# Selective scan: the sum over states on TensorE as accumulating transposes, and relu in place in PSUM

## The chip, the core and the metric

The kernel runs on one core of a Trainium2 chip. The metric is the device time of one execution in microseconds (us), as the median of several runs. The core's engines work side by side, each through its own queue of instructions in order: TensorE (PE in the profile, with PEld for its weight loads), VectorE (DVE), ScalarE (ACT), GpSimd (POOL) and SyncE (SP), which issues nearly all DMAs here. SBUF is the on-chip memory of 128 partitions; PSUM is the smaller memory that TensorE writes its results to.

## The reference, cut to what matters

Four layers work on x of 256 x 256 positions and 128 channels. Layer 1 holds the selective scan that the change is about: for each of 4 directions k, 256 inner channels d and 16 states n, a recurrence over all L = 65536 positions.

```python
delta = jax.nn.softplus(dts + dt_bias[None, :, :, None])
def step(h, inp):
    d_t, x_t, B_t, C_t = inp
    dA = jnp.exp(d_t[..., None] * As)
    h = dA * h + (d_t * x_t)[..., None] * B_t[:, :, None, :]
    y = jnp.einsum('bkdn,bkn->bkd', h, C_t)
    return (h, y)
...
return ys + Ds[None, :, :, None] * xs
```

y is thus a sum over the 16 states of h times C, plus a multiple of x. The directions are row by row, column by column, and each of these backwards; their outputs are added later.

## The kernel before, in words

The scans (`scan_stream`, L577) come third in the kernel: layer 0 and a convolution come before them, the layer's end, layer 2 and layer 3 after. The work is cut into N = 512 chunks of CH = 512 positions, 128 for each direction. Channels lie on partitions, in two halves dh = 0 and 1. A chunk has NG = 8 steps s, one group g of scans each: s % 2 is the half dh, and s // 2 picks G = 4 of the 16 states.

What one group needs, and who does it:

- `scans` (L770): twice per group, ACT computes the two exponentials of a pair of states (L786) into one of two PSUM buffers `das`, corrects the column at the seam of the pair with the state kept from the chunk before (L790), and DVE runs one scan over 1024 elements (L801) into the SBUF tile h, of which there are 3. After the first scan of a group ACT keeps the last group's states (`keep_state`, L812).
- `b_product` (L768): delta times x times B, on POOL for j in (2, 4, 6), else on DVE. The table `b_order` says in which step each stands.
- `c_product` (L816): POOL multiplies h by C into hc, of which there are 3.
- `sums` (L829 to 837): TensorE adds up the states. Four matmuls per group with the identity as the stationary operand accumulate hc[:, i] in the PSUM tile ys[dh], 128 x 512. A matmul in fp32 is two PE instructions in the trace. `y_start` (L819) opens the accumulation with the multiple of x (directions 0, 1) or with the output of the opposite direction (2, 3). `sums(g - 2)` stands after the scans of group g.
- `y_out` (L844): ACT copies the finished ys[dh] to the block yo in SBUF, which a DMA stores.

The next chunk's delta is made beside this in one PSUM tile, mm, first for dh = 0 and then for dh = 1: `xproj` (L672) and `dt` (L704) are matmuls; `soft_abs` (L716, L717) takes |v| and relu(v) from mm to SBUF; `soft_exp` (L723, L724) turns |v| into log(1 + exp(-|v|)); `soft_sum` (L730) adds the two parts in mm with two identity matmuls; `delta_copy` (L738) takes the result to SBUF; `delta_x` (L746) multiplies it by x on DVE; `du_copy` (L757) keeps a copy for POOL.

The order is written by hand under `manual_schedule`. Small pieces of ACT work, the "extras", are put behind the first (extras[0]) or the second scan (extras[1]) of a step; ACT's queue is in order, so extras[0] stands ahead of the exponentials of the step's second scan. In step 1 extras[1] is soft_abs and y_out of half 0 of the chunk before; in step 2 extras[0] is soft_exp and extras[1] is y_out of half 1.

The attention of layer 0 uses 128x128 fp32 transposes on TensorE (L341), with the data as the stationary operand and the identity streaming.

Of the kernel before, what the change touches and what calls it, by code (L numbers as in the profile page):

```python
# [10 lines left out]
F32 = mybir.dt.float32  # L11
AF = mybir.ActivationFunctionType
# [5 lines left out]
P = 128  # L18
S = 256
NPOS = S * S  # L20
CH = 512
# [555 lines left out]
def scan_stream(c, xc2, y, w):  # L577
# [7 lines left out]
    tc, nc = c.tc, c.nc  # L585
    G, BL, NG = 4, 1024, 8
# [8 lines left out]
    N = len(chunks)  # L595
    with ExitStack() as a:
# [3 lines left out]
        wk = a.enter_context(tc.tile_pool(name="l1b_wk", bufs=2))  # L600
# [9 lines left out]
        ys = [ps1.tile([P, CH], F32, name=f"l1b_y{dh}") for dh in range(2)]  # L610
# [2 lines left out]

        mm = ps1.tile([P, CH], F32, name="l1b_mm")
        du1 = ps1.tile([P, CH], F32, name="l1b_du")
        blocks, bcs, bbs, ccs, soft, dls, dbs, hs, hcs = ({} for _ in range(9))

        def cols(ch):
            return bass.ds(chunks[ch][1] * CH % BL, CH)

        def in_block(yo, ch, dh):

            k, i = chunks[ch]
            if k % 2 == 0:
                return yo[:, dh, cols(ch)]
            v = yo[:, dh].rearrange("p (b w r) -> p w b r", w=NW, r=R)
            return v[:, bass.ds(i * CH % BL // S, CH // S)]

        def like_block(ap, ch):

            if chunks[ch][0] % 2 == 0:
                return ap
            return ap.rearrange("p (w b r) -> p w b r", b=S // R, r=R)

        def block_dma(far, k, i, yo, store):
            b = i * CH // BL
            if k % 2 == 0:
                pairs = [(far[:, bass.ts(b, BL)].rearrange("(h p) t -> p h t", p=P), yo)]
            else:
                pairs = [  # L640
                    (
                        far[h * P : h * P + P, :, bass.ts(b, NW)].rearrange("p b w r -> p b (w r)"),
                        yo[:, h].rearrange("p (b m) -> p b m", m=NW * R),
                    )
                    for h in range(2)
                ]
            for there, here in pairs:
                nc.sync.dma_start(*((there, here) if store else (here, there)))

        def load_x(ch):  # L650

            if ch >= N:
                return
            k, i = chunks[ch]
            xc = io.tile([P, 2, BL], F32, name="l1b_xc")
            block_dma(xc2[k % 2], k, i, xc, False)
            blocks[ch] = blocks[ch + 1] = [xc, None]

        def load_y(ch):
            if ch >= N:  # L660
                return
            k, i = chunks[ch]
            yo = blocks[ch][1] = io.tile([P, 2, BL], F32, name="l1b_yo")
            if k >= 2:
                block_dma(y[k - 2], k, i, yo, False)
# [46 lines left out]
        def soft_abs(ch):  # L712
            if ch >= N:
                return
            soft[ch] = [wk.tile([P, CH], F32, name=f"l1b_{n}", bufs=1) for n in ("tail", "relu")]
            nc.scalar.activation(soft[ch][0], mm, AF.Abs)  # L716
            nc.scalar.activation(soft[ch][1], mm, AF.Relu)  # L717

        def soft_exp(ch):
            if ch >= N:  # L720
                return
            tail = soft[ch][0]
            nc.scalar.activation(tail, tail, AF.Exp, scale=-1.0)  # L723
            nc.scalar.activation(tail, tail, AF.Ln, bias=1.0)  # L724

        def soft_sum(ch):
            if ch >= N:
                return
            for i, part in enumerate(soft.pop(ch)):
                nc.tensor.matmul(mm, c.ident, part, start=i == 0, stop=i == 1)  # L730

        def delta_copy(ch, dh):

            if ch >= N:
                return
            k = chunks[ch][0]
            dl = dls[ch, dh] = wk.tile([P, CH], F32, name=f"l1b_dl{dh}")
            nc.scalar.copy(dl, mm)  # L738
            af = dls[ch, dh, "first"] = wk.tile([P, 16], F32, name=f"l1b_af{dh}")
            t0 = CH - 1 if k >= 2 else 0  # L740
            nc.scalar.activation(af, w["A"][:, k, dh], AF.Exp, scale=dl[:, t0 : t0 + 1])

        def delta_x(ch, dh):
            if ch >= N:
                return
            nc.vector.tensor_tensor(  # L746
                like_block(du1 if dh else mm, ch),
                like_block(mm, ch),
                in_block(blocks[ch][0], ch, dh),
                ALU.mult,  # L750
            )
# [7 lines left out]
        def b_product(g):  # L759
            ch, j = divmod(g, NG)  # L760
            if ch >= N:
                return
            db = dbs[g] = wk.tile([P, G, CH], F32, name="l1b_db", bufs=5)
            if j in on_pool:
                eng, du = nc.gpsimd, dls[ch, "du"]
            else:
                eng, du = nc.vector, du1 if j % 2 else mm
            eng.tensor_tensor(db, bbs[g // 2], du[:, None, :].to_broadcast([P, G, CH]), ALU.mult)  # L768
# [47 lines left out]
            nc.gpsimd.tensor_tensor(hc, hs[g], ccs[g // 2], ALU.mult)  # L816
            hs.pop(g - 1, None)

        def y_start(ch, dh):  # L819
            k = chunks[ch][0]  # L820
            xc, yo = blocks[ch]
            if k >= 2:
                nc.tensor.matmul(ys[dh], c.ident, in_block(yo, ch, dh), start=True, stop=False)
            else:
                nc.tensor.matmul(
                    ys[dh], w["dsum"][:, k, dh], in_block(xc, ch, dh), start=True, stop=False
                )

        def sums(g):  # L829
            ch, j = divmod(g, NG)  # L830
            if j < 2:
                y_start(ch, j)
            hc = hcs.pop(g)
            for i in range(G):
                nc.tensor.matmul(  # L835
                    ys[j % 2], c.ident, hc[:, i], start=False, stop=j // 2 * G + i == 15
                )

        def y_out(ch, dh):
            if ch < 0:  # L840
                return
            k, i = chunks[ch]
            yo = blocks[ch][1]
            nc.scalar.copy(in_block(yo, ch, dh), like_block(ys[dh], ch))  # L844
            if dh == 1 and ch % 2 == 1:
                block_dma(y[k], k, i, yo, True)
# [23 lines left out]
        for ch in range(N):  # L870
            nxt = ch + 1
            for s in range(NG):
                g = NG * ch + s
                if s == 3 and ch % 2 == 0:
                    load_y(ch + 2)
                if s == 5 and ch % 2 == 1:
                    load_x(ch + 3)
                if s == 4:
                    delta_x(nxt, 0)
                for j in b_order.get(s, ()):  # L880
                    b_product(NG * ch + j)
                extras = [[], []]
                if s == 1:
                    extras[1] = [lambda: soft_abs(nxt), lambda: y_out(ch - 1, 0)]
                if s == 2:
                    extras = [[lambda: soft_exp(nxt)], [lambda: y_out(ch - 1, 1)]]
                if s == 3:
                    extras[1] = [lambda: delta_copy(nxt, 0)]
                if s == 4:
                    extras[0] = [lambda: du_copy(nxt)]  # L890
                if s == 5:
                    extras = [[lambda: soft_abs(nxt)], [lambda: soft_exp(nxt)]]
                if s == 6:
                    extras[1] = [lambda: xd_copy(ch + 2)]
                if s == 7:
                    extras[0] = [lambda: delta_x(nxt, 1), lambda: b_product(g + 2)]
                    extras[1] = [lambda: delta_copy(nxt, 1)]
                if s == 0:
                    dt(nxt, 0)
                scans(g, extras)  # L900
                if s == 2:
                    soft_sum(nxt)
                if s == 4:
                    dt(nxt, 1)
                if s == 5:
                    xproj(ch + 2)
                if s == 6:
                    soft_sum(nxt)
                if g >= 2:
                    sums(g - 2)  # L910
                c_product(g)
                if s % 2 == 1:
                    load_b(g // 2 + 4)
                    load_c(g // 2 + 3)
        keep = N * NG
        sums(keep - 2)
        y_out(N - 1, 0)
        sums(keep - 1)
        y_out(N - 1, 1)


def scan_weights(c, pool, w):
# [830 lines left out]
```

## Time and profile before

| what | value |
|---|---|
| median of 3 runs | 34197.11 us (34196.43 to 34205.05) |
| span of the profiled execution | 34210.0 us |
| mean granted TensorE clock of the whole run | 0.927 |
| stretch 4000 to 16600 us: DVE busy | 12281.89 of 12600 us |
| the same stretch: POOL busy | 12442.54 us |
| the same stretch: ACT busy | 8882.16 us |
| the same stretch: PE busy | 10557.95 us, clock 0.92 |
| L835 (sums), PE | 16063.1 us, 32768 instructions |
| L844 (y_out), ACT copy PSUM to SBUF, 128x512 | 558 to 586 ns, 1024 times |

The profile is of one execution. A group of instructions has its line in kernel.py, engine, operation, output and inputs, count, busy time and mean duration, then the engine's idle time just before its instructions and what ended most of it. In a list of waits, a line reads: the waiting engine and line, the releaser, total us, times, the longest. In a timeline: start, duration, engine, line, operation, output and inputs, how many in a row were merged, and in brackets idle time and its releaser. The granted clock is the share of TensorE's full clock that its throttle let through; 0.5 is half rate. The scans fill the time from 3.9 to 29.5 ms, three quarters of the span.

### The profile page before, as it was taken

What the parts mean: (1) busy time and instruction counts of PE and PEld (TensorE: products, weight loads), DVE (VectorE), ACT (ScalarE), POOL (GpSimd) and SP (SyncE); (2) the same over time, 40 slices, a digit from 0 to 9 for tenths busy, and PEclk for the clock granted to TensorE, in tenths of its full rate; (3) what the DMA queues carried; (4) which work ended last, traced back from release to release, by engine and by line L of the source; (5) the groups of instructions that cost most, each with busy time, mean ns of one, the idle gap of its engine ahead of it and who ended that gap; (6) DMA issues with size and microseconds to landing.
All of it is one profiled execution on the core that took longest, in us unless ns stands there. A gap on an engine that the chain in (4) does not pass through costs nothing. (4 is left out here: it accounts for less than half of the span.)

```text
span 34210.0 us, 256813 instructions
## 1 busy us (share of the span) xinstructions
PE 28944.2 (85%) x72308; PEld 12107.5 (35%) x72308; DVE 31098.5 (91%) x23680; ACT 22856.5 (67%) x47119; POOL 27441.3 (80%) x6996
## 2 busy tenths in 40 slices
PE   7999888888888888888888888888888888899877
PEld 3554333333333333333333333333333333334444
DVE  6668999999999999999999999999999999863699
ACT  3667777777777777777777777777777777532477
POOL 2446899999999999999999999999999999620000
PEclk9999999999999999999999999999999999999999
DMA  3113455545555555555555555555555555675111
GB/s 142 45 45 123 181 191 189 191 190 193 190 191 190 191 189 191 191 190 192 196 202 200 202 199 203 201 201 203 201 201 201 200 201 201 210 234 157 66 35 33
DMA packets 2076530, 5947.88 MB, mean 174 GB/s; under 512 B 115207, under 2 KB 1379608, under 8 KB 1499222
## 3 DMA queue, kind: packets, MB, share of 16 engines
q1 hardware_dynamic: 1939122, 5860.18, 46.9%
q10 hardware_dynamic: 135972, 71.27, 0.7%
q8 instruction: 570, 9.34, 0.1%
q14 instruction: 866, 7.09, 0.1%
HBM read 5238.41 MB, written 692.58 MB: 173 GB/s over the span
## 5 line engine op out<-in xcount | busy, mean ns | idle before, releaser
L801 DVE TENSOR_TENSOR_SCAN l1b_h<-l1b_da,l1b_state,l1b_db 128x1024 f32<-128x1024 f32 x8192 | 18793.3, 2336 | 597.1 <-ACT l1b_db L790 586.1
L816 POOL TENSOR_TENSOR l1b_hc<-l1b_h,l1b_cc 128x2048 f32<-128x2048 f32 x4096 | 18452.2, 4530 | 325.9 <-DVE l1b_h L801 324.9
L835 PE MATMUL l1b_y<-l1b_hc,ident 128*128 128x512 f32 x32768 | 16063.1, 639 | 1119.3 <-POOL l1b_hc L816 1119.2
L786 ACT ACTIVATE l1b_da<-l1b_dl,l_alog 128x512 f32<-128x512 f32 (+1 forms) x16384 | 11296.5, 689 | 3153.8 <-DVE l1b_h L801 2845.9
L835 PEld LDWEIGHTS l1b_y<-l1b_hc,ident 128*128 128x128 f32 x32768 | 6529.4, 205 | 10693.4 <-issue 8166.8
L768 POOL TENSOR_TENSOR l1b_db<-l1b_bb,l1b_dus 128x2048 f32<-128x2048 f32 x1536 | 6969.8, 4538 | 46.0 <-DMA l1b_bb<-l1b_bc 46.0
L768 DVE TENSOR_TENSOR l1b_db<-l1b_bb,l1b_du 128x2048 f32<-128x2048 f32 x2048 | 4658.6, 2275 | 35.2
L790 ACT ACTIVATE l1b_db<-l1b_state,l1b_db,l1b_af 128x1 f32<-128x1 f32 x8192 | 3045.1, 372 | 0.0
L704 PE MATMUL l1b_mm<-l1b_xd,l_dtw 41*128 41x512 f32 x2048 | 1372.7, 755 | 1703.2 <-ACT l1b_dus L757 1697.4
L730 PE MATMUL l1b_mm<-l1b_tail,ident 128*128 128x512 f32 x2048 | 1294.8, 718 | 1382.6 <-ACT l1b_tail L724 1380.1
L812 ACT COPY l1b_state<-l1b_h 128x4 f32<-128x4 f32 x4095 | 789.4, 193 | 2433.7 <-DVE l1b_h L801 2433.6
L332 POOL TENSOR_TENSOR l0b_e<-l0b_e,l0b_den 128x1024 f32<-128x1024 f32 x512 | 969.9, 1894 | 1373.6 <-DVE l0b_den L331 729.4
L730 PE MATMUL l1b_mm<-l1b_relu,ident 128*128 128x512 f32 x2048 | 1310.3, 728 | 0.0
L704 PEld LDWEIGHTS l1b_mm<-l1b_xd,l_dtw 41*128 41x128 f32 x2048 | 338.0, 206 | 2517.8 <-ACT l1b_dus L757 2120.5
L757 ACT COPY l1b_dus<-l1b_mm 128x512 f32<-128x512 f32 x512 | 300.2, 586 | 1388.3 <-DVE l1b_db L768 1387.8
L768 DVE TENSOR_TENSOR l1b_db<-l1b_bb,l1b_mm 128x2048 f32<-128x2048 f32 x512 | 1171.6, 2288 | 18.2 <-ACT l1b_dus L757 0.7
L308 DVE CUSTOM_DVE_ANT_0 l0b_e<-l0b_sc,l0b_bias 128x256 f32<-128x256 f32 x2048 | 745.5, 421 | 415.6 <-PE l0b_sc L297 412.2
L730 PEld LDWEIGHTS l1b_mm<-l1b_tail,ident 128*128 128x128 f32 x2048 | 377.3, 207 | 2053.9 <-ACT l1b_tail L724 1805.5
L323 ACT ACTIVATE l0b_e<-l0b_e,l0b_top 128x256 f32<-128x256 f32 x2048 | 1012.0, 498 | 0.9 <-DVE l0b_top L308 0.9
L672 PE MATMUL l1b_du<-l1b_xc,l_xproj 128*40 128x512 f32 x2048 | 981.6, 602 | 32.3 <-DMA l1b_xc<-l_xc 31.5
L738 ACT COPY l1b_dl<-l1b_mm 128x512 f32<-128x512 f32 x1024 | 588.3, 574 | 524.7 <-DVE l1b_du L746 516.9
L986 POOL TENSOR_TENSOR l1c_y<-l1c_y,l1c_yt 128x512 f32<-128x512 f32 x256 | 396.8, 1572 | 600.0 <-DMA l1c_y<-l_y 558.0
(278 smaller groups left out, 29961.9 us busy)
## 6 DMA issues: line engine op xcount, KB each, us to landing
l1b_bb<-l1b_bc SPq DMA_DIRECT2D x2048, 1024.0 KB
l1b_cc<-l1b_bc SPq DMA_DIRECT2D x2048, 1024.0 KB
l1b_xc<-l_xc SPq DMA_DIRECT2D x128, 1024.0 KB
l_y<-l1b_yo SPq DMA_DIRECT2D x128, 1024.0 KB
l1b_xc<-l_xct SPq DMA_DIRECT2D x256, 512.0 KB
l_y<-l1b_yo SPq DMA_DIRECT2D x256, 512.0 KB
l_xc<-l1a_o SPq DMA_DIRECT2D x64, 1024.0 KB
l_xct<-l1a_ot SPq DMA_DIRECT2D x16, 4096.0 KB
```

What stands on the lines that cost most here:

```text
L323: nc.scalar.activation(e[:, i], e[:, i], AF.Exp, scale=-1.0, bias=top[:, i : i + 1], accum_out=den[:, i : i + 1],)
L332: nc.gpsimd.tensor_tensor(e, e, den[:, :, None].to_broadcast([P, 4, S]), ALU.mult)
L672: nc.tensor.matmul(du1[:40], w["xproj"][:, dh, k, :], in_block(blocks[ch][0], ch, dh), start=dh == 0, stop=dh == 1,)
L704: nc.tensor.matmul(mm, w["dt"][:, chunks[ch][0], dh * P : dh * P + P], xds[ch % 3][0:41], start=True, stop=True,)
L730: nc.tensor.matmul(mm, c.ident, part, start=i == 0, stop=i == 1)
L768: eng.tensor_tensor(db, bbs[g // 2], du[:, None, :].to_broadcast([P, G, CH]), ALU.mult)
L786: nc.scalar.activation(da[:, o + lo : o + hi], dl[:, lo:hi], AF.Exp, scale=w["A"][:, k, dh, n : n + 1])
L790: nc.scalar.activation(first, states[k][:, dh, two : two + 1], AF.Identity, scale=af[:, two : two + 1], bias=first,)
L801: nc.vector.tensor_tensor_scan(h_, a_, d_, states[k][:, dh, one : one + 1], ALU.mult, ALU.add)
L812: nc.scalar.copy(states[k][:, dh, n0 : n0 + G], hs[g][:, :, 0 if k >= 2 else CH - 1])
L816: nc.gpsimd.tensor_tensor(hc, hs[g], ccs[g // 2], ALU.mult)
L835: nc.tensor.matmul(ys[j % 2], c.ident, hc[:, i], start=False, stop=j // 2 * G + i == 15)
```

## The change

The states are now summed as transposes. Each 128x128 block of hc is the stationary operand and the identity streams, in transpose mode, and the results accumulate in ys, which so holds the transposed sum. Once per chunk and half, ACT copies it to SBUF (`y_turn`); TensorE then opens ys anew with the multiple of x, or the opposite direction's output, and adds the four blocks turned back by transposes (`y_back`); y_out follows as before. `y_start` at the head of the sums is gone. y_turn and y_back stand in extras[0] of steps 1 and 2, and soft_exp for dh = 0 moves from extras[0] to extras[1] of step 2.

For softplus, relu is written in place to mm in PSUM in place of an SBUF tile, and soft_sum adds only the logarithm's part to it, with one matmul in place of two.

```diff
         def soft_abs(ch):
...
-            soft[ch] = [wk.tile([P, CH], F32, name=f"l1b_{n}", bufs=1) for n in ("tail", "relu")]
-            nc.scalar.activation(soft[ch][0], mm, AF.Abs)
-            nc.scalar.activation(soft[ch][1], mm, AF.Relu)
+            soft[ch] = wk.tile([P, CH], F32, name="l1b_tail", bufs=1)
+            nc.scalar.activation(soft[ch], mm, AF.Abs)
+            nc.scalar.activation(mm, mm, AF.Relu)
...
-            for i, part in enumerate(soft.pop(ch)):
-                nc.tensor.matmul(mm, c.ident, part, start=i == 0, stop=i == 1)
+            nc.tensor.matmul(
+                mm, c.ident, soft.pop(ch), start=False, stop=True, skip_group_check=True
+            )
...
-        def y_start(ch, dh):
+        def y_turn(ch, dh):
+            if ch < 0:
+                return
+            yt = yts[dh] = wk.tile([P, CH], F32, name="l1b_yt", bufs=1)
+            nc.scalar.copy(yt, ys[dh])
+
+        def y_back(ch, dh):
+            if ch < 0:
+                return
             k = chunks[ch][0]
             xc, yo = blocks[ch]
             if k >= 2:
-                nc.tensor.matmul(ys[dh], c.ident, in_block(yo, ch, dh), start=True, stop=False)
+                nc.tensor.matmul(ys[dh], c.ident, in_block(yo, ch, dh), start=True, stop=True)
             else:
                 nc.tensor.matmul(
-                    ys[dh], w["dsum"][:, k, dh], in_block(xc, ch, dh), start=True, stop=False
-                )
+                    ys[dh], w["dsum"][:, k, dh], in_block(xc, ch, dh), start=True, stop=True
+                )
+            for b in range(CH // P):
+                turned(ys[dh], b, yts[dh][:, bass.ts(b, P)], False, True)
+
+        def turned(to, b, part, start, stop):
+            nc.tensor.matmul(
+                to[:, bass.ts(b, P)],
+                part,
+                c.ident,
+                start=start,
+                stop=stop,
+                is_transpose=True,
+                skip_group_check=True,
+            )
 
         def sums(g):
             ch, j = divmod(g, NG)
-            if j < 2:
-                y_start(ch, j)
             hc = hcs.pop(g)
             for i in range(G):
-                nc.tensor.matmul(
-                    ys[j % 2], c.ident, hc[:, i], start=False, stop=j // 2 * G + i == 15
-                )
+                n = j // 2 * G + i
+                for b in range(CH // P):
+                    turned(ys[j % 2], b, hc[:, i, bass.ts(b, P)], n + b == 0, n == 15)
...
                 if s == 1:
-                    extras[1] = [lambda: soft_abs(nxt), lambda: y_out(ch - 1, 0)]
+                    extras = [
+                        [lambda: y_turn(ch - 1, 0), lambda: y_back(ch - 1, 0)],
+                        [lambda: soft_abs(nxt), lambda: y_out(ch - 1, 0)],
+                    ]
                 if s == 2:
-                    extras = [[lambda: soft_exp(nxt)], [lambda: y_out(ch - 1, 1)]]
+                    extras = [
+                        [lambda: y_turn(ch - 1, 1), lambda: y_back(ch - 1, 1)],
+                        [lambda: soft_exp(nxt), lambda: y_out(ch - 1, 1)],
+                    ]
...
-        sums(keep - 2)
-        y_out(N - 1, 0)
-        sums(keep - 1)
-        y_out(N - 1, 1)
+        for dh in range(2):
+            sums(keep - 2 + dh)
+            y_turn(N - 1, dh)
+            y_back(N - 1, dh)
+            y_out(N - 1, dh)
```

## The prediction

> **What bounds the kernel now.** I read the page first (busy shares, slices, costliest groups), then the waits inside the scan stage, then the timeline of one chunk, engine by engine.
>
> ```profile
> PE 28944.2 (85%) x72308; PEld 12107.5 (35%) x72308; DVE 31098.5 (91%) x23680; ACT 22856.5 (67%) x47119; POOL 27441.3 (80%) x6996
> L801 DVE TENSOR_TENSOR_SCAN l1b_h<-l1b_da,l1b_state,l1b_db 128x1024 f32<-128x1024 f32 x8192 | 18793.3, 2336 | 597.1 <-ACT l1b_db L790 586.1
> L816 POOL TENSOR_TENSOR l1b_hc<-l1b_h,l1b_cc 128x2048 f32<-128x2048 f32 x4096 | 18452.2, 4530 | 325.9 <-DVE l1b_h L801 324.9
> L835 PE MATMUL l1b_y<-l1b_hc,ident 128*128 128x512 f32 x32768 | 16063.1, 639 | 1119.3 <-POOL l1b_hc L816 1119.2
> ```
>
> The groups with l1b_ in their names run from 3.9 to 29.5 ms: 512 equal chunks. Successive chunks start their last product of VectorE (DVE) at 15001.61 and 15051.55, so one takes 49.94 us; a stage table over that stretch has DVE busy 48.68, GpSimd (POOL) 49.33, TensorE (PE) 43.97 and ScalarE (ACT) 35.20 us. The waits say who follows whom:
>
> ```profile
> DVE l1b_h L801 <- ACT l1b_db L790: 580.2, 1019, 1.8
> POOL l1b_hc L816 <- DVE l1b_h L801: 303.2, 507, 4.6
> POOL l1b_hc L816 <- PE l1b_y L835: 1.0, 1, 1.0
> ```
>
> POOL waits for DVE once a chunk (0.6 us), DVE never for POOL or PE; DVE waits only for ACT, twice a chunk. So a chunk lasts as long as DVE's 48.7 us of work plus ACT's delays of it (about 1.13 us). PE, whose work the change halves, holds up nobody: its sums wait for POOL. What can move the time is ACT's queue between two scans. There ACT writes two exponentials (L786) into one of two PSUM buffers and corrects one column (L790); then the scan may start. In s = 1, whose queue the change alters (t is the time after 15000 us):
>
> ```profile
> 15012.87 0.20 ACT L812 COPY l1b_state<-l1b_h 128x4 f32<-128x4 f32 x1 [0.52 <-DVE l1b_h L801]
> 15012.97 1.41 ACT L786 ACTIVATE l1b_da<-l1b_dl,l_alog 128x512 f32<-128x512 f32 x2
> 15014.32 0.37 ACT L790 ACTIVATE l1b_db<-l1b_state,l1b_db,l1b_af 128x1 f32<-128x1 f32 x1
> 15014.99 2.33 DVE L801 TENSOR_TENSOR_SCAN l1b_h<-l1b_da,l1b_state,l1b_db 128x1024 f32<-128x1024 f32 x1
> ```
>
> L790 ends at t = 14.69, the scan starts at 14.99. In s = 5 two activations (L716, L717) already stand there:
>
> ```profile
> 15038.40 0.20 ACT L812 COPY l1b_state<-l1b_h 128x4 f32<-128x4 f32 x1 [0.64 <-DVE l1b_h L801]
> 15038.50 0.59 ACT L716 ACTIVATE l1b_tail<-l1b_mm 128x512 f32<-128x512 f32 x1
> 15038.99 0.59 ACT L717 ACTIVATE l1b_relu<-l1b_mm 128x512 f32<-128x512 f32 x1
> 15039.47 1.42 ACT L786 ACTIVATE l1b_da<-l1b_dl,l_alog 128x512 f32<-128x512 f32 x2
> 15040.82 0.37 ACT L790 ACTIVATE l1b_db<-l1b_state,l1b_db,l1b_af 128x1 f32<-128x1 f32 x1
> 15041.23 2.35 DVE L801 TENSOR_TENSOR_SCAN l1b_h<-l1b_da,l1b_state,l1b_db 128x1024 f32<-128x1024 f32 x1 [0.62 <-ACT l1b_db L790]
> ```
>
> A 128x512 activation takes 0.59 us but moves the next start by 0.48; L790's end is followed by the scan 0.04 us later; DVE idles 0.62.
>
> **What the skill says.** "TensorE: Matmul & The Clock Gate", Part 4: a transpose is one matmul with the data as an operand, about 275 ns in a kernel, and it does not count as TensorE activity as a matmul does, so the full clock does not engage. The trace agrees on the price: the transposes of the attention (L341, also fp32) have a median of 273 ns. The same page, Part 1, has the clock at half rate until a window of about 3.4 us is busy; here matmul groups that follow an idle 2.88 us run at half rate:
>
> ```profile
> 15019.09 2.07 PE L730 MATMUL l1b_mm<-l1b_tail,ident 128*128 128x512 f32 x2 [2.88 <-ACT l1b_tail L724]
> 15020.96 1.92 PE L730 MATMUL l1b_mm<-l1b_relu,ident 128*128 128x512 f32 x2
> ```
>
> "ScalarE: Activation LUTs", Step-by-step, holds that PSUM is ScalarE's nearer destination. The trace has no activation from PSUM to PSUM; its exponentials from SBUF take 0.69 us into PSUM, 0.62 into SBUF (L723).
>
> **The change, part by part.** A line of transposes, in both clocks:
>
> ```profile
> 577.51 1.97 PE L341 MATMUL l0b_tp<-ident,l0b_e 128*128 128x128 f32 x8 [2.45 <-POOL l0b_e L332]
> 579.41 2.08 PE L297 MATMUL l0b_sc<-l0b_k,l0b_q 32*128 32x256 f32 x8
> 591.63 1.09 PE L341 MATMUL l0b_tp<-ident,l0b_e 128*128 128x128 f32 x8
> ```
>
> *Sums.* Eight take 1.09 us at full clock; less the last one's 0.272, a start-to-start of 0.82/7 = 0.117 us. At half clock 1.97 and, for the last, 0.476 give 0.213. A group's sums, before 8 half-products 0.43 apart (3.70 us with the tail), become 16 transposes: 15 x 0.117 + 0.27 = 2.03 us, or 15 x 0.213 + 0.48 = 3.67. Per chunk PE's work is then 8 x 2.03 + two turns back of 1.33 + soft, dt and xproj of 1.7 each = 24 us at full clock, 45 at half (before: 44). No wait of DVE's goes away with that: it is worth 0. The cover if PE falls behind is POOL's pace: a product hc comes every 4.5 us or slower.
>
> *Soft sum* loses one of its two matmuls (0.85 us per half): DVE's delta product reads the result at t = 30.7, the sum ends by t = 22.7; worth 0.
>
> *Relu in place* (L717): no instruction more, output to PSUM. In s = 5 it stands on DVE's path. Bounds: 0.05 us shorter (its step of 0.48 cannot go far below the 512 elements' flow), 0.10 longer (0.69 against 0.59). I take 0.
>
> *y_turn, dh = 0.* A new copy in s = 1, between L812 and L786, priced like L844 (next start 0.47 to 0.48 later; both read y in PSUM). Exponentials at 12.97 + 0.48 = 13.45, L790 at 14.80 to 15.17, scan at 15.21 in place of 14.99: **+0.22 us**. The same from s = 5: 0.96 us of activations there cost 0.71 from start to start, a slack of 0.25 or 0.26, and 0.48 - 0.26 = 0.22. Nothing behind catches it up, since all of DVE's later work follows. y itself is ready: its last product ends at 8.0, the transposes by 11.7 even at half clock.
>
> *y_back, dh = 0.* PE waits for the copy (13.54, so 13.6), then a 512 matmul and four transposes. In PE's in-order queue stand behind it the sums of dh = 1 (product ready since 12.45), y_back of dh = 1, the soft sum. Half clock: 1.71 + 0.85 to the next start, 16.16, sums until 16.16 + 3.67 = 19.83. Full clock: 14.93, then 16.96. y_out waits at 16.05 for the turn back, at half clock till 16.47; the exponentials for s = 2 then end with L790 at 18.68, ahead of their scan (19.41 + 0.22), so that costs 0.
>
> *y_turn, dh = 1,* in s = 2, takes the place of soft_exp (1.19 us to 0.48), which goes one scan later. At full clock it runs at 18.27, L790 ends at 20.47, and the scan (21.67 + 0.22 = 21.89) is on time. It stays so up to a copy at 19.65. At half clock the copy waits for PE until 19.88: exponentials 20.36, L790 21.71 to 22.08, scan 22.12: **+0.23 us**. soft_exp and the second y_out then end by 24.1, the next exponentials' L790 by 25.9, and their scan comes at 26.7: covered, also because DVE's product stands ahead of it. The delta copy moves from 25.8 to 27.5 and is wanted at 31.
>
> *Rest.* No DMA is added or moved; the output's store follows y_out by a fraction of a microsecond. The last chunk's two extra turns add a few microseconds once.
>
> **Sum.** Half clock: 512 x (0.22 + 0.23) = 230 us on the profiled span, 34210 + 230 = 34440; that span is 13 us above the median of the runs, so 34427. Full clock: 512 x 0.22 = 113, giving 34310.
>
> **Rivals.** *Half clock in that stretch (forecast, 0.45):* for it, PE's idle time grows, a 2.88 us gap already drops the clock, and the transposes and narrow matmuls from 577.5 to 590 ran 13 us without a gap before the clock rose, while the full-size matmuls from 15019.1 needed 5.7. *Full clock, or a sum done by 19.6 (0.30):* 34310; for it, the same mix held the clock once risen; the margin is 0.23 us of a 6.2 us stretch. *PE or ACT short of time (0.12):* with PE at 45 of 50 us, relu 0.10 longer and another 0.2 in s = 2, 512 x 0.75 = 384: 34580, and more if PE's queue backs up. *Not slower (0.13):* half of PE's reads of hc go, and if that made DVE's instructions faster, 23 of them a chunk would pay the 0.22 back from 10 ns each on. Against it: the product at 15017.23 takes 2.27 us with PE idle, the one at 15006.07 2.26 with PE busy. A relu step shorter by 0.05 would add 26 us to that. It gives 34197 with 10 ns.
>
> **How the numbers follow.** A measurement of this kernel tells about 0.2% (68 us) from no change. Slower: 0.45 + 0.30 + 0.12, less 0.01 for the full clock with every bound at its best = 0.86; the last rival and that rest split into same 0.10 and faster 0.04. The range starts at the full clock with a copy step of 0.43 and the shorter relu, 512 x 0.12 = 61, so about 34255, and ends just above the third case, 34600; most of the last rival (0.13) lies outside.
>
> **What would show it.** Right: DVE's waits for L790 rise from two to three or four a chunk, the new ones in s = 1 (about 0.2) and s = 2; a new wait of ACT's l1b_yt for PE, about 1.2 us a chunk; clock near 0.5 to 0.6 in the slices where it is 0.9; POOL's wait for DVE grows as much as DVE's. Wrong: no wait of DVE's in s = 1, or scans and products of another length, or waits of POOL's for PE.

## The result, and the profile after

The changed kernel takes 35855.31 us in the median (35851.63 to 35861.86), the kernel before in the same comparison 34198.96: a ratio of 1.0483, 95% interval 1.0468 to 1.0498. It is slower by 1656 us, seven times the 230 forecast. The profiled execution spans 35859.9 us.

From the page of the changed kernel, busy time by engine and three of the costliest groups (lines 738 to 816 of before are now one higher; the sums are L841):

```profile
PE 23526.7 (66%) x107124; PEld 15174.0 (42%) x107124; DVE 31172.5 (87%) x23680; ACT 23389.7 (65%) x48143; POOL 27460.8 (77%) x6996
...
L802 DVE TENSOR_TENSOR_SCAN l1b_h<-l1b_da,l1b_state,l1b_db 128x1024 f32<-128x1024 f32 x8192 | 18851.5, 2337 | 681.0 <-ACT l1b_db L791 590.4
...
L841 PE MATMUL l1b_y<-ident,l1b_hc 128*128 128x128 f32 x65536 | 10401.2, 326 | 5510.9 <-POOL l1b_hc L817 5506.4
...
L769 DVE TENSOR_TENSOR l1b_db<-l1b_bb,l1b_du 128x2048 f32<-128x2048 f32 x2048 | 4660.6, 2276 | 1531.9 <-DMA l1b_bb<-l1b_bc 1496.7
```

PE's busy time fell from 28944 to 23527 us, and DVE's is what it was (31098 to 31172). The scans keep their length, 2337 ns, and their idle time rises by 84 us only. The last line is the loss: the products of DVE now wait 1497 us for the DMA that brings B (l1b_bb), where they waited for nothing. The page's slices say when:

```profile
DVE  6668888888888888888899999999999999883599
...
PEclk9999877777777777777777878788778777899999
```

DVE is below nine tenths busy in the first half of the scans, and back in the second, while the clock is low in both. The halves are directions 0 and 1, and directions 2 and 3. The waits over the scans (4.0 to 30.9 ms; total us, times, longest):

```profile
DVE l1b_db L769 <- DMA l1b_bb<-l1b_bc: 1496.7, 128, 13.6
POOL l1b_db L769 <- DMA l1b_bb<-l1b_bc: 1496.2, 128, 13.6
...
DVE l1b_h L802 <- ACT l1b_db L791: 580.1, 1003, 1.8
POOL l1b_hc L817 <- DVE l1b_h L802: 434.4, 506, 4.8
ACT l1b_yt L824 <- PE l1b_y L841: 122.7, 251, 1.1
```

128 waits of nearly 12 us each: as many as there are blocks of two chunks in directions 0 and 1 (125 of them lie before 18 ms). SyncE's own waits name the cause:

```profile
SPq L648 <- PE l1b_y L834: 2085.6, 68, 35.1
SPq L648 <- PE l1b_y L841: 1850.4, 64, 32.0
```

L648 is `block_dma`, the load of x or of an older y, and the store of y; L834 is the matmul of y_back that multiplies x, and L841 all the transposes. The list puts down the waits of direction 0 to L834 and nearly all of direction 1 to L841; the timeline of direction 1 below shows the load going out at the end of an L834 there too. In the kernel before, L648 hardly waited for PE (the longest such wait was 0.7 us):

```profile
SPq L648 <- PE l1b_y L835: 39.3, 79, 0.5
```

One of the stalls, in the timelines of SyncE, PE and DVE:

```profile
14980.56 0.32 SPq L698 DMA_DIRECT2D l1b_cc<-l1b_bc  x1
15010.79 1.29 SPq L648 DMA_DIRECT2D l1b_xc<-l_xct  x2
15012.18 0.60 SPq L692 DMA_DIRECT2D l1b_bb<-l1b_bc  x1
```

```profile
15009.63 1.12 PE L834 MATMUL l1b_y<-l1b_xc,l_dsum 128*128 128x512 f32 x2 [1.99 <-ACT l1b_yt L824]
```

```profile
14998.98 9.31 DVE L802 TENSOR_TENSOR_SCAN l1b_h<-l1b_da,l1b_state,l1b_db 128x1024 f32<-128x1024 f32 x4
15020.70 2.29 DVE L769 TENSOR_TENSOR l1b_db<-l1b_bb,l1b_du 128x2048 f32<-128x2048 f32 x1 [12.41 <-DMA l1b_bb<-l1b_bc]
```

The load of the next x block is issued 0.04 us after the L834 that ends at 15010.75. It overwrites the buffer (there are two) whose last reader that matmul is. It had stood at the head of SyncE's queue for some 30 us: the load of C before it went out at 14980.56. The load of B behind it lands when DVE has been idle for 12.41 us.

In the kernel before, y_start read x at the head of the chunk's own sums, so the buffer was free in step 5 of the odd chunk, where `load_x` stands. y_back reads it in steps 1 and 2 of the *next* chunk. In directions 2 and 3 it reads yo instead, and there is no stall.

The other term is also in this timeline: four scans in a row take 9.31 us. In the kernel before they took 9.07:

```profile
15008.25 9.07 DVE L801 TENSOR_TENSOR_SCAN l1b_h<-l1b_da,l1b_state,l1b_db 128x1024 f32<-128x1024 f32 x4
```

From one chunk to the next (waits of step 5 at 15044.74 and 15094.94) it is 50.20 us without a stall, 0.26 more than before. Together, 1497 + 512 x 0.26 = 1630 of the 1656 us; the other 26 stay open.

### The profile page after: what moved, and what is told of

Same layout as the page of the kernel before. It is cut to its first block, busy times and chain, and to the rows that moved or that the text cites. A ratio compares the mean times of both kernels' runs of the same rounds, so it can differ in the third digit from the quotient of the medians.

```text
span 35859.9 us, 328109 instructions
## 1 busy us (share of the span) xinstructions
PE 23526.7 (66%) x107124; PEld 15174.0 (42%) x107124; DVE 31172.5 (87%) x23680; ACT 23389.7 (65%) x48143; POOL 27460.8 (77%) x6996
## 5 line engine op out<-in xcount | busy, mean ns | idle before, releaser
L802 DVE TENSOR_TENSOR_SCAN l1b_h<-l1b_da,l1b_state,l1b_db 128x1024 f32<-128x1024 f32 x8192 | 18851.5, 2337 | 681.0 <-ACT l1b_db L791 590.4
L787 ACT ACTIVATE l1b_da<-l1b_dl,l_alog 128x512 f32<-128x512 f32 (+1 forms) x16384 | 11301.8, 690 | 4184.0 <-DVE l1b_h L802 3875.9
L841 PE MATMUL l1b_y<-ident,l1b_hc 128*128 128x128 f32 x65536 | 10401.2, 326 | 5510.9 <-POOL l1b_hc L817 5506.4
L841 PEld LDWEIGHTS l1b_y<-ident,l1b_hc 128*128 128x128 f32 x65536 | 9483.5, 172 | 8015.5 <-POOL l1b_hc L817 6409.9
L704 PE MATMUL l1b_mm<-l1b_xd,l_dtw 41*128 41x512 f32 x2048 | 1739.9, 943 | 3492.8 <-ACT l1b_dus L758 2889.8
L704 PEld LDWEIGHTS l1b_mm<-l1b_xd,l_dtw 41*128 41x128 f32 x2048 | 435.4, 264 | 3778.3 <-ACT l1b_dus L758 3026.9
L729 PE MATMUL l1b_mm<-l1b_tail,ident 128*128 128x512 f32 x2048 | 1109.8, 624 | 633.4 <-ACT l1b_tail L724 630.9
L832 PE MATMUL l1b_y<-l1b_yo,ident 128*128 128x512 f32 x1024 | 716.5, 788 | 814.0 <-ACT l1b_yt L824 814.0
L834 PE MATMUL l1b_y<-l1b_xc,l_dsum 128*128 128x512 f32 x1024 | 710.6, 782 | 818.8 <-ACT l1b_yt L824 818.8
L672 PE MATMUL l1b_du<-l1b_xc,l_xproj 128*40 128x512 f32 x2048 | 1155.7, 692 | 32.2 <-DMA l1b_xc<-l_xc 31.4
L841 PEld LDWEIGHTS l1b_y<-ident,l1b_yt 128*128 128x128 f32 x4096 | 652.2, 172 | 722.7 <-issue 722.7
```

The costliest lines, as they stand in the source:

```text
L672: nc.tensor.matmul(du1[:40], w["xproj"][:, dh, k, :], in_block(blocks[ch][0], ch, dh), start=dh == 0, stop=dh == 1,)
L704: nc.tensor.matmul(mm, w["dt"][:, chunks[ch][0], dh * P : dh * P + P], xds[ch % 3][0:41], start=True, stop=True,)
L729: nc.tensor.matmul(mm, c.ident, soft.pop(ch), start=False, stop=True, skip_group_check=True)
L787: nc.scalar.activation(da[:, o + lo : o + hi], dl[:, lo:hi], AF.Exp, scale=w["A"][:, k, dh, n : n + 1])
L802: nc.vector.tensor_tensor_scan(h_, a_, d_, states[k][:, dh, one : one + 1], ALU.mult, ALU.add)
L841: nc.tensor.matmul(to[:, bass.ts(b, P)], part, c.ident, start=start, stop=stop, is_transpose=True, skip_group_check=True,)
```

## The experiments

Theory A: the late read of x holds its buffer, `load_x` holds SyncE's queue, and B is late; the rest is y_turn's copy in ScalarE's queue. Theory B: TensorE's lower clock, or the DMA traffic of its many instructions, makes things late. Each kernel is compared with runs of the kernel before on the same chip: 34203.79 us for experiments 1, 2, 3 and 6, 34198.09 for 4, 34195.77 for 5 and 7.

**1. after_load_late.** Only the place of the load is changed.

```diff
-        load_x(2)
...
                 if s == 3 and ch % 2 == 0:
+                    load_x(ch + 2)
                     load_y(ch + 2)
-                if s == 5 and ch % 2 == 1:
-                    load_x(ch + 3)
```

> The changed kernel, with the load of the next x block issued in step 3 of the even chunk (behind the turn back that reads the old block last) in place of step 5 of the odd chunk. Theory A (the load waits in SyncE's queue for the last turn back's read of the old block, and the loads of B behind it come late): the 12.4 us waits of VectorE and GpSimd for l1b_bb, 128 of them, are gone, some 1500 us; what stays is 0.26 us a chunk, 512 x 0.26 = 133, so about 34330. Theory B (TensorE's lower clock, or the DMA traffic of its doubled instructions, makes things late): the order of the loads doesn't matter, about 35850. If A holds only in part, between the two.

34356.64 us, ratio 1.0045 (1.0028 to 1.0061). The waits for l1b_bb are gone, and with them 1499 us. The clock is nearly as low as without that edit (0.838 over the run against 0.820), and the transposes are as many: theory B falls for the large term.

**2. before_late_reader.** The converse: the suspected cause alone, put into the kernel before.

```diff
+        last = st.tile([P, 1], F32, name="l1b_last")
+
+        def touch(ch):
+            if ch >= 0 and chunks[ch][0] < 2:
+                nc.scalar.copy(last, blocks[ch][0][:, 1, BL - 1 : BL])
...
                 if s == 2:
-                    extras = [[lambda: soft_exp(nxt)], [lambda: y_out(ch - 1, 1)]]
+                    extras = [[lambda: soft_exp(nxt), lambda: touch(ch - 1)], [lambda: y_out(ch - 1, 1)]]
```

> The kernel before, plus one ScalarE copy of a 128x1 column of the x block of the chunk before, in step 2 behind soft_exp, in directions 0 and 1 only: a late reader of that block, at about the time at which the changed kernel's last turn back reads it; TensorE is left as it was. Theory A: the load of x is held until that copy (about 20 us later), and 128 waits for l1b_bb of 11 to 13 us appear: 34197 + 128 x 12 = about 35730. Theory B: one small copy, which has cover there, so about 34200.

35541.57 us, ratio 1.0391 (1.0375 to 1.0406): 1338 us, from a copy of one column. DVE's waits for B, and one stall in DVE's timeline:

```profile
DVE l1b_db L768 <- DMA l1b_bb<-l1b_bc: 1318.5, 128, 12.3
```

```profile
15031.05 9.07 DVE L801 TENSOR_TENSOR_SCAN l1b_h<-l1b_da,l1b_state,l1b_db 128x1024 f32<-128x1024 f32 x4
15051.60 2.29 DVE L768 TENSOR_TENSOR l1b_db<-l1b_bb,l1b_du 128x2048 f32<-128x2048 f32 x1 [11.48 <-DMA l1b_bb<-l1b_bc]
```

The four scans are at 9.07 again: the stall and the small term are separate. The mean wait is 1318.5 / 128 = 10.3 us, not 12. In the stalls shown, the copy ends 10.9 us after the start of the four scans and the last matmul of x in the changed kernel 11.8 us after it, which explains part of the difference.

**3. before_load_late.** The control: experiment 1's edit on the kernel before.

> The kernel before, with the load of the next x block in step 3 of the even chunk, as a control: it has no late reader, so both theories expect no change, 34200 within 0.2%. If it is faster or slower, the same shift in the other kernel has to be corrected by it.

34199.15 us, ratio 0.9999 (0.9991 to 1.0008). The move is worth nothing by itself.

**4. after_load_behind_step5 and after_load_behind_step7.** What is late, x or what stands behind it? The load keeps its wait and is only put behind the loads of B and C of step 5, or of step 7.

```diff
-                if s == 5 and ch % 2 == 1:
-                    load_x(ch + 3)
...
                     load_b(g // 2 + 4)
                     load_c(g // 2 + 3)
+                if s == 5 and ch % 2 == 1:
+                    load_x(ch + 3)
```

> The changed kernel with the load of x in the same step 5 of the odd chunk, but issued behind that step's loads of B and C instead of ahead of them; the wait for the last turn back stays. Theory (what stalls VectorE is not x, but the loads of B held behind it in SyncE's queue): the load of B for groups 4 and 5 is no longer held, but the next one, for groups 6 and 7, is: it is issued about 14 us after the chunk's start and wanted at 18, and lands some 7 to 8 us after its issue: 3 to 4 us a block, 34350 + 128 x 3.5 = about 34800. Rival (x itself comes too late for its users): no better than the changed kernel, 35850.

34991.87 us, ratio 1.0233 (1.0216 to 1.025).

> The changed kernel with the load of x issued behind the loads of B and C of step 7. Theory: the loads of B that the next chunk wants are all ahead of it, and x itself is in time for xproj in step 5: no stall, about 34350. Rival (x is late): as above, 35850.

34342.1 us, ratio 1.0043 (1.0028 to 1.0058). In the first, one load of B moved ahead of x, and the stall falls to this:

```profile
DVE l1b_db L769 <- DMA l1b_bb<-l1b_bc: 634.8, 128, 7.1
```

```profile
14981.47 2.29 DVE L769 TENSOR_TENSOR l1b_db<-l1b_bb,l1b_du 128x2048 f32<-128x2048 f32 x1 [6.87 <-DMA l1b_bb<-l1b_bc]
```

5.0 us a block where 3.5 were expected: the next B load is still held. For the stall shown it goes out at 14974.41, 0.2 us before DVE wants it and not 4, and lands 7 us later, as expected. With step 7's loads ahead too, there is no stall. In all three orders the timelines near 15 ms have x issued 0.03 to 0.04 us after the last L834 that reads the old block, so it is the queue behind it that costs, and not x.

**5. before_relu_in_psum and before_relu_and_copy.** The small term, taken apart in the kernel before: first relu in place and the shorter soft_sum (the diff is that part of the change), then y_turn's copy alone, to a tile that nobody reads.

```diff
+        def y_copy(ch):
+            if ch >= 0:
+                nc.scalar.copy(wk.tile([P, CH], F32, name="l1b_yt", bufs=1), ys[0])
...
-                    extras[1] = [lambda: soft_abs(nxt), lambda: y_out(ch - 1, 0)]
+                    extras = [[lambda: y_copy(ch - 1)], [lambda: soft_abs(nxt), lambda: y_out(ch - 1, 0)]]
```

> The kernel before with the softplus part of the change alone: relu in place in PSUM, soft_sum with one matmul. The wait in step 5 was 0.62 us before and 0.64 in the changed kernel. Theory: 512 x 0.02 = 10 us more, so 34200 to 34215, no change within 0.2%. Rival: the shorter soft_sum is worth something to VectorE, below 34130; or the relu into PSUM costs its full 0.1 us in step 5, 34250.

34205.92 us, ratio 1.0003 (0.9994 to 1.0011): no change; the wait in step 5 is 0.64 us for 0.62.

> The same, plus one ScalarE copy of y of half 0 to an SBUF tile that nobody reads, at the place of y_turn in step 1, behind the first scan. TensorE's sums stay the 512-wide matmuls, and nothing is turned back. Theory (the small term is the copy's place in ScalarE's queue): 0.22 to 0.24 us more a chunk, 512 x 0.23 = 118, about 34325. Rival (the small term comes from TensorE): as without the copy, about 34205.

34377.29 us, ratio 1.0051 (1.0034 to 1.0068). In its timelines, ACT's copy and DVE's four scans:

```profile
15031.24 0.58 ACT L842 COPY l1b_yt<-l1b_y 128x512 f32<-128x512 f32 x1
15031.72 1.42 ACT L787 ACTIVATE l1b_da<-l1b_dl,l_alog 128x512 f32<-128x512 f32 x2
```

```profile
15026.52 9.31 DVE L802 TENSOR_TENSOR_SCAN l1b_h<-l1b_da,l1b_state,l1b_db 128x1024 f32<-128x1024 f32 x4
```

The copy moves the exponentials by 0.48 us and the scan by 0.24, with TensorE's sums left as they were: 171 us over the relu part alone, where 118 were expected. 123 of it is 512 x 0.24. The list of waits has 37 us of this copy for PE's sums (71 times); if all of it reached DVE, 11 us stay unexplained. A chunk in this timeline lasts 50.20 us, as in the changed kernel.

**6. after_turn_moved.** With experiment 1's load, half 0's turn goes behind step 1's second scan.

```diff
                 if s == 1:
-                    extras = [
-                        [lambda: y_turn(ch - 1, 0), lambda: y_back(ch - 1, 0)],
-                        [lambda: soft_abs(nxt), lambda: y_out(ch - 1, 0)],
-                    ]
+                    extras[1] = [
+                        lambda: y_turn(ch - 1, 0),
+                        lambda: y_back(ch - 1, 0),
+                        lambda: soft_abs(nxt),
+                    ]
                 if s == 2:
                     extras = [
-                        [lambda: y_turn(ch - 1, 1), lambda: y_back(ch - 1, 1)],
+                        [lambda: y_out(ch - 1, 0), lambda: y_turn(ch - 1, 1), lambda: y_back(ch - 1, 1)],
```

> The changed kernel with the late load, and y_turn and y_back of half 0 moved in step 1 from behind the first scan to behind the second, y_out of half 0 from step 1 to the head of step 2. Theory A with its small term (0.22 to 0.26 us a chunk is the copy of y ahead of the second scan's exponentials of step 1): that wait is gone, 34197 + 512 x 0.02 = about 34210. If the small term is TensorE's (late sums, lower clock), it stays near 34330 or grows, since half 0's turn back comes later.

34838.15 us, ratio 1.0186 (1.0171 to 1.0201): a miss, by 630 us. The timelines of PE, ACT and DVE:

```profile
15028.56 2.07 PE L834 MATMUL l1b_y<-l1b_xc,l_dsum 128*128 128x512 f32 x2 [4.17 <-ACT l1b_yt L824]
15030.43 1.06 PE L841 MATMUL l1b_y<-ident,l1b_yt 128*128 128x128 f32 x4
15031.28 2.68 PE L841 MATMUL l1b_y<-ident,l1b_hc 128*128 128x128 f32 x16
```

```profile
15034.00 0.59 ACT L824 COPY l1b_yt<-l1b_y 128x512 f32<-128x512 f32 x1 [1.88 <-PE l1b_y L841]
```

```profile
15021.60 9.07 DVE L802 TENSOR_TENSOR_SCAN l1b_h<-l1b_da,l1b_state,l1b_db 128x1024 f32<-128x1024 f32 x4
...
15036.24 2.35 DVE L802 TENSOR_TENSOR_SCAN l1b_h<-l1b_da,l1b_state,l1b_db 128x1024 f32<-128x1024 f32 x1 [1.13 <-ACT l1b_db L791]
```

The four scans are at 9.07: the wait of step 1 is gone, as expected. By the time alone, the rival would have won: it expected the loss to grow. But PE takes half 0's turn up later, after 4.17 us idle and at half clock; half 1's sums stand behind it, ACT's second copy waits 1.88 us for them, and the scan of step 2 waits 1.13. The edit thus put a loss of TensorE's in the place of the copy's, and says nothing on whose the small term was; experiment 5 does. This is the chain that the prediction priced at 0.23; it opens when the first turn comes later.

**7. before_product_moved and after_late_product_moved.** DVE's product for group 7 goes from step 3 to between the scans of step 5, where DVE waits for ACT. The second run does it in the changed kernel with experiment 1's load.

```diff
-    b_order = {0: (3,), 1: (4,), 2: (5,), 3: (6, 7), 4: (8,), 6: (10,)}
+    b_order = {0: (3,), 1: (4,), 2: (5,), 3: (6,), 4: (8,), 6: (10,)}
...
                 if s == 5:
-                    extras = [[lambda: soft_abs(nxt)], [lambda: soft_exp(nxt)]]
+                    extras = [[lambda: soft_abs(nxt), lambda: b_product(g + 2)], [lambda: soft_exp(nxt)]]
```

> The kernel before with VectorE's product for group 7 moved from the head of step 3 to between the two scans of step 5, where VectorE waits 0.62 and then 0.51 us for ScalarE. If the waits are what they look like, both go (1.3 us a chunk from start to start), until GpSimd sets the pace with its 49.3 us: 49.94 to 49.4, 512 x 0.54 = 276 less, about 33930. If a wait of the same size opens in steps 3 and 4, about 34200.

33874.66 us, ratio 0.9906 (0.9891 to 0.992).

> The changed kernel with the late load of x, and the same product moved. VectorE's waits of step 5 and 6 go, that of step 1 (0.24) stays, and GpSimd sets the pace: again 49.4 a chunk, about 33930, so that the change's small term is hidden behind GpSimd. If ScalarE's longer extras of step 2 (soft_exp and y_out) now reach the scan of step 3, which has no product ahead of it any more, or the late sums hold ScalarE, 34050 to 34350.

33901.24 us, ratio 0.9914 (0.9899 to 0.9928). Both beat both kernels, and lie within 27 us of each other, less than the width of either interval. The waits of the first show why it ends there:

```profile
DVE l1b_h L801 <- ACT l1b_db L790: 203.4, 316, 1.8
DVE l1b_du L746 <- PE l1b_mm L730: 145.1, 127, 1.3
...
POOL l1b_hc L816 <- DVE l1b_h L801: 2.1, 2, 1.8
```

DVE's waits for ACT fall from 580 to 203 us, and POOL no longer waits for DVE (303 us before): from 5 to 15 ms it is busy 10000 of 10000 us in both, where it was 9875. POOL now sets the pace, and what the change adds on ACT is nearly hidden behind it. In the first of the two, DVE has a new wait for PE, in softplus (145 us); the second has none, but ends no sooner, since POOL leads. The kernel before with one product moved has the lowest time of all.

## Why the prediction was wrong, point by point

*What bounds the kernel:* right. DVE's work plus ACT's delays of it make the chunk; taking a fifth off PE's busy time, with the stall taken away, gave nothing (34357 against 34204).

*y_turn, dh = 0:* right, and the right size: +0.22 a chunk predicted, 0.24 measured (9.31 against 9.07), and shown by experiment 5 to be ACT's copy. Its sign was misjudged: the list of waits leaves out so short a gap (DVE's waits for ACT stay at two a chunk, 1003), and it shows only from start to start. In the chunk from 15061.70 the last two of the four scans take 4.80 us, the two in the middle 4.57. *Relu in place:* 0 taken, 0.02 measured.

*Half clock, y_turn of dh = 1:* 0.23 predicted, next to nothing measured in the changed kernel: PE's clock went to half only in parts (0.78 over the scans, not 0.5 to 0.6), and ACT's copies waited 123 us for PE, 251 times in all, where 1.2 us in each of 512 chunks were forecast. The chunk's 0.26 is the copy and the relu. So the time of the second clock case came nearer, though not its full clock; with the load mended, the loss is 153 us against its 113. The chain itself exists, as experiment 6 shows.

*The step that failed* is the one on y_back, dh = 0, with the Rest: "No DMA is added or moved". y_back was followed forward, to what stands behind it on PE. It was not asked what the moved matmul *reads*. It reads the x block, whose release moved with it by most of a chunk; `load_x`, unmoved in the text, therefore moved in time, and with it every load behind it in SyncE's queue. That term was 0 in the sum and measured 1497 us, nine tenths of the loss. No rival had it. The marks of it were there before: two buffers of l1b_xc in the kernel, and loads of x, B and C from one queue, SPq, in the page's table of DMA issues.

## What to carry to other kernels

When an operation is moved later, list its inputs as well as its output: each input's buffer is released later, and the transfer that refills it waits at the head of its queue with all that stands behind. Put a load whose buffer is freed late behind the loads that others want sooner, or issue it after its last reader. And before an engine is relieved, look whether anyone waits for it: here one product moved into the place where DVE waits was worth 321 us, and a third less time in TensorE's sums (10174 us of L841 in experiment 1 against 16063 of L835 before) nothing.

## What the runs showed of the hardware that was not expected

Groups of 16 fp32 transposes ran in 1.91 to 1.97 us at full clock and 3.67 at half, where 2.03 and 3.67 were estimated from the attention's groups of 8; but the clock did engage with them. The Trainium skill, "TensorE: Matmul & The Clock Gate", Part 4, says that the full clock does not engage for transposes. These runs show that it can, and the measurement decides. The 16 transposes from 15061.16 of the changed kernel follow 4.34 us of idle PE; the clock is 0.50 up to 15063.50 and 1.00 from 15064.00, with nothing else on PE. With those from 15142.81, after 14.23 us idle, it rises after about 3 us; other groups of 16 end before it does. In the chunk from 15061.70 it stood at 1.00 for 15072 to 15082 and 15097 to 15107, through groups of which most of the work is transposes. It fell to 0.50 within idle stretches of 4.34 and 6.04 us and just after one of 2.61. The 275 ns that the prediction takes from that part is given there for bf16, so the attention's 273 ns in fp32 is no test of it.

Relu in place in PSUM lasts as long as relu to SBUF (L717: median 587 ns in both kernels), and moved the next start by 0.51 us where SBUF took 0.48 (L717 to L787 in step 5); this step shows no gain from PSUM as a destination. The exponentials that the prediction compares, 0.69 us into PSUM and 0.62 into SBUF, differ in their scale too, a column of A against the constant -1, so they do not single out the destination.
